# The first pair of blocks from half tables: loads into them, gathers by halves, and the next loads moved to GpSimd

## The chip, the cores and the metric

The kernel runs on one core of a Trainium2 chip. The metric is the device time of one execution in microseconds (us). Before the change three runs gave 733.4, 733.51 and 733.7; the median is 733.51. One further execution, under the profiler, took 733.14 with a span of 731.4 between its first and last instruction. All times below without a unit are microseconds from the start of that span.

## The reference: three layers of products of fields

The input x has 1024 rows of 39 fields with 64 numbers each. With X0 = x, each of three layers forms, for every row b and number e,

```
Xk_next[b, o, e] = sum over h, f of  Xk[b, h, e] * X0[b, f, e] * W[o, h, f]  +  bias[o]
```

with 64 outputs o. Each layer's result is summed over e, the three sums are put in a row of 192, and one linear layer (fc_w, fc_b) gives one number for each of the 1024 rows. Everything is float32.

The first layer has X0 twice, so its sum runs over pairs of fields. Because only sums over e and a linear layer follow, the last two layers are folded into weights beforehand: what is left for the large data is the first layer with its folded neighbour (128 output columns), a product with the first layer's result, and sums.

## The kernel before

**Blocks.** x is cut into 32 blocks of 32 rows. A block has 2048 columns (32 rows times 64 numbers) and one table row for each field, so it is a table of 39 rows of 8 KB, and a fortieth row of ones, which lets a single field pass as a product. Two blocks are a pair and share a DRAM table `xd[k]` of 80 rows (FT = 40 for each block); three such tables are used in turn.

**Gathers.** Products of all pairs of fields are made by multiplying differently ordered copies of the table. For each block, five tiles of 128 rows (`rt[n % 2]`, tiles 0 to 4) are filled with table rows in the orders that `lists` holds, one indirect DMA for each tile, issued by GpSimd (`gather_rows`, L174; called r in the profile). For each pair of blocks two smaller tiles, `ut` and `vt`, of 128 rows by 1024 columns, hold the few pairs of fields that the large tiles leave out (`roll_small`). Their 128 rows are four groups of 32, one for each combination of block and half of the columns.

**Products and matmuls.** Six products of tiles, numbered by `PAIRS = ((0, 1), (0, 2), (3, 1), (3, 2), (0, 4), (3, 4))`, are made by VectorE for each block (L219, `product`), each 128 by 2048, and one u by v product (L221) for each pair of blocks. TensorE multiplies each with its weights and sums into four PSUM banks for each block (L559, `multiply`). The u by v product is spread over both blocks by small matmuls (L579 and L590, `join`), between the two blocks of a pair. VectorE runs up to four products ahead of TensorE, with four buffers.

**Finishing a block.** `finish` takes the four banks: ScalarE copies one half and adds a column of fc_w (L607), VectorE adds the bias `b0s` and multiplies (L609), and sums over e (L620). In VectorE's order the finish of block 0 stands after product 3 of block 1 and ahead of product 4.

**Order of the queues.** Each engine runs its own instructions in the order in which the program lists them. An instruction waits until the tiles and DRAM rows that it needs are there; what stands behind it waits too. [...]

**The first pair.** The first block is handled by halves of 1024 columns. ScalarE's queue loads the halves of block 0 into `xh[0]` and `xh[1]` (39 rows each). GpSimd gathers tiles 0 to 3 of block 0 from them, eight half gathers, and among them issues the load of block 1 into `xd[0]`. SP copies both halves into `xd[0]` (L396). Tile 4, which needs the row of ones, u, v and the tiles of block 1 are gathered from `xd[0]`. Then GpSimd issues small loads of biases, b0s first (L477), and a row of ones. SP loads blocks 2 and 3 once TensorE's first step is in order, and later blocks 6 and up; GpSimd loads blocks 4 and 5 behind the gathers of blocks 2 and 3.

**The start.** Before the first product is used, TensorE, VectorE and ScalarE prepare the folded weights, up to the first L559 at 17.34.

Of the kernel before, what the change touches and what calls it, by code (L numbers as in the profile page):

```python
# [54 lines left out]
F32 = mybir.dt.float32  # L55
# [92 lines left out]
def cin_kernel(ctx: ExitStack, tc: tile.TileContext, x, w0t, b0, w1, b1, w2, b2, fc_w, fc_b, out):  # L148
# [11 lines left out]
    xd = [dram.tile([2 * FT, BLK], F32, name=f"xd{k}") for k in range(NTAB)]  # L160
    xh = [dram.tile([F, SUB], F32, name=f"xh{k}") for k in range(2)]

# [9 lines left out]

    def gather_rows(dst, table, k):
        nc.gpsimd.indirect_dma_start(  # L174
            dst, None, table, bass.IndirectOffsetOnAxis(ap=lists[:, k : k + 1], axis=0)
        )

    def roll(n, tiles=range(NT)):
# [4 lines left out]
    def roll_small(n):  # L183
        table = xd[n // 2 % NTAB].rearrange("f (t c) -> (f t) c", c=SUB)
        for k, dst in enumerate((ut, vt)):
            gather_rows(dst[n // 2 % 2], table, 2 * NT + k)

# [12 lines left out]

    lists = const.tile([128, 2 * NT + 2], I32, name="lists")
    rt = [const.tile([128, NT, BLK], F32, name=f"r{k}") for k in range(2)]
# [22 lines left out]
    with prep as prep:  # L225
# [25 lines left out]
        def load_half(k):  # L251
            nc.scalar.dma_start(
                xh[k].rearrange("f (b e) -> b f e", e=E), x[k * SB : (k + 1) * SB]
            )
# [34 lines left out]

        tmp = prep.tile([128, 16], F32, name="tmp")  # L290
        wide = prep.tile([128, 5, NT], F32, name="wide")
# [78 lines left out]

        fill_ones(0, nc.gpsimd, ones)


        nc.vector.tensor_scalar(unit, apart, 0, None, ALU.is_equal)
        for h in (0, H):
# [3 lines left out]
            )  # L379
        r, most, seat, far = (new() for _ in range(4))  # L380
        both_of = prep.tile([128, 2], F32, name="both_of")
# [7 lines left out]
        halves = [slice(0, SUB), slice(SUB, BLK)]  # L389
        for k, cols in enumerate(halves):  # L390
            for i in range(4):
                gather_rows(rt[0][:, i, cols], xh[k], i)
                if k and i == 1:
                    load(1, nc.gpsimd)
        for k in (1, 0):
            nc.sync.dma_start(xd[0][0:F, halves[k]], xh[k])  # L396
        roll(0, (4,))

# [31 lines left out]
        fused(seat, row, 96.0, seat, ALU.is_ge, ALU.add)  # L430
        step(row, 64.0, 2.0 * FT - 1.0, far)
        nc.vector.tensor_reduce(jumps, steps_at, AX.X, ALU.add)
# [28 lines left out]
        for k, n in enumerate((8, 5)):  # L461
            for t in range(2):
# [6 lines left out]
                )  # L469
        nc.vector.tensor_tensor(seat, seat, far, ALU.add)  # L470
        nc.vector.tensor_tensor(both_of[:, 0:1], most, jumps[:, 0:1], ALU.add)
        nc.vector.tensor_tensor(both_of[:, 1:2], both_of[:, 0:1], jumps[:, 1:2], ALU.add)
        nc.vector.tensor_scalar(lists[:, 2 * NT :], both_of, 2.0, seat, ALU.mult, ALU.add)
        roll_small(0)
        roll(1)
        for h in (0, H):
# [5 lines left out]
        )  # L482
        fill_ones(2, nc.gpsimd, ones)
        w1v = w1s.rearrange("o (h f) -> o h f", f=F)
# [82 lines left out]
    def join(n, p):  # L567
        open_block(n + 1)

        def tiles(t, side):  # L570
            rows = slice(SQUARE * t, SQUARE * t + SQUARE)
            return rows, po[n + t // 2][2 * t % 4 + side]

        for side in range(2):
            for t in range(4):
                for half in range(2):
                    rows, dst = tiles(t, side)
                    at = (side + half) * H
                    nc.tensor.matmul(  # L579
                        dst[half * H : half * H + H],  # L580
                        wa[rows, NPAIR, at : at + H],
                        p[rows, bass.ts(side, MM)],
                        start=t >= 2,
                        stop=t < 2 and half == side,
                    )
        for t in range(4):
            for side in range(2):
                rows, dst = tiles(t, side)
                half = (1 - side) * H
                nc.tensor.matmul(  # L590
                    dst[half : half + H],
                    wa[rows, NPAIR + 1, H : 2 * H],
                    ut[n // 2 % 2][rows, bass.ts(side, MM)],
                    start=False,
                    stop=t < 2,
                )
# [92 lines left out]
    for at, (n, c) in enumerate(steps[:-TAIL]):  # L689
        if c == 0 and 2 <= n and n + 4 < NBLK:  # L690
            load(n + 4)
# [15 lines left out]
        if not at:  # L707
            fields(0)
            nc.scalar.copy(ones1, ones)
            fill_ones(1, nc.sync, ones1)  # L710
            for k in (2, 3):
                load(k)
        if at == NPAIR - 2:
# [6 lines left out]
        if at + AHEAD < len(steps):  # L720
            n, c = steps[at + AHEAD]
            if at + AHEAD <= NPAIR:
                weight_rows(c)
            p[n, c] = product(n, c)
            if c == NPAIR - 1 and n + 2 < NBLK:
                roll(n + 2)
                if n % 2 == 0:
                    roll_small(n + 2)
                if n < 2:
                    load(n + 4, nc.gpsimd)  # L730
# [75 lines left out]
```

## Time and profile before

| What | Value |
|---|---|
| median of three runs | 733.51 us (733.4 to 733.7) |
| the profiled execution | 733.14 us, span 731.4 us |
| TensorE matmul busy | 724.7 us, 99% |
| VectorE busy | 638.3 us, 87% |
| GpSimd busy | 397.6 us, 54% |
| DMA moved | 197.24 MB, mean 270 GB/s |
| gathers from `xd` into r | 156, mean 1938 ns of GpSimd each |
| half gathers from `xh` into r | 8, mean 996 ns each |
| direct loads of a block by GpSimd | 3, mean 1055 ns each |

Busy time is the time in which an engine has an instruction in work; a share of 99% means that the engine hardly stood still. In the lists of instructions a row gives the start, how long it took, the engine (PE is TensorE, DVE is VectorE, ACT is ScalarE, POOL is GpSimd), the line of the program, the operation, what it writes and reads, and in brackets how long the engine was idle ahead of it and what ended that. "issue" there is time in which the profile shows nothing that the engine waits for. A group of a page has the count after x, then busy time and the mean of one in ns, then the idle time ahead.

### The profile page before, as it was taken

The numbers are of one execution on the slowest core, as the hardware profiler recorded it, in microseconds if no ns is written. First come the engines' busy times: TensorE is split into PE (matmuls) and PEld (weight loads), VectorE is DVE, ScalarE is ACT, GpSimd is POOL, SyncE is SP. The second block draws the span as 40 slices with busy tenths as digits, with TensorE's granted clock in tenths as the row PEclk, the third lists the DMA queues.
The fourth block names the chain that finished last, engine by engine and source line by source line (L and its number), as shares of the span: only waits on it lengthen the run. The fifth ranks groups of instructions, "written<-read, shape, count | busy, mean of one in ns | idle before, by whom it ended". The sixth has DMA issues, their size and how long they took to land.

```text
span 731.4 us, 6351 instructions
## 1 busy us (share of the span) xinstructions
PE 724.7 (99%) x2375; PEld 316.1 (43%) x2375; DVE 638.3 (87%) x521; ACT 166.9 (23%) x240; POOL 397.6 (54%) x254
## 2 busy tenths in 40 slices
PE   8999999999999999999999999999999999999998
PEld 4444444444444444444444444444444444444443
DVE  6999798988889988889988889888898988889885
ACT  3332121222212222221222212222121221212222
POOL 6789886536555445754537555455654547545300
PEclk9999999999999999999999999999999999999999
DMA  8997899789575887757679675896767777565700
GB/s 268 376 337 280 315 342 356 290 307 338 232 273 231 281 336 286 270 225 285 269 288 330 223 289 219 304 348 236 268 256 274 301 287 266 224 252 236 288 0 0
DMA packets 65983, 197.24 MB, mean 270 GB/s; under 512 B 40110, under 2 KB 40179, under 8 KB 45984
## 3 DMA queue, kind: packets, MB, share of 16 engines
q0 software_dynamic: 28784, 185.56, 65.5%
q1 hardware_dynamic: 35468, 9.29, 5.5%
q10 hardware_dynamic: 1700, 1.99, 1.0%
q8 instruction: 18, 0.29, 0.1%
q14 instruction: 13, 0.11, 0.0%
HBM read 196.76 MB, written 10.60 MB: 284 GB/s over the span
## 4 chain that ended last, share of the span: by engine, by line
PE 99%; DVE 0%; DMA 0%; issue 0%; ACT 0%; DVEq 0%
PE po L559 91%; PE po L579 4%; PE po L590 2%; PE idle L279 0%; PE pv L406 0%; PE pt L487 0%; PE small L323 0%; PE pv L487 0%; PE pw L418 0%; DMA fcrow<-in_fc_w 0%; PE tr L543 0%; DVE g L609 0%; DVE pairs L526 0%; DVE sums L631 0%; ACT z L607 0%
## 5 line engine op out<-in xcount | busy, mean ns | idle before, releaser
L559 PE MATMUL po<-p,wa 128*128 128x512 f32 x1536 | 666.0, 594 | 0.0
L219 DVE TENSOR_TENSOR p<-r 128x2048 f32<-128x2048 f32 (+2 forms) x198 | 434.1, 2224 | 72.4 <-PE po L559 67.1
L559 PEld LDWEIGHTS po<-p,wa 128*128 128x128 f32 x1536 | 290.5, 190 | 371.7 <-issue 354.6
L174 POOL DMA_INDIRECT r<-xd,lists x156 | 302.3, 1938 | 267.1 <-issue 266.2
L607 ACT ACTIVATE z<-po,columns 64x512 f32<-64x512 f32 x128 | 87.3, 682 | 380.1 <-PE po L590 217.9
L609 DVE SCALAR_TENSOR_TENSOR g<-po,b0s,z 64x512 f32<-64x512 f32 x128 | 95.9, 749 | 9.3 <-ACT z L607 5.3
L602 ACT COPY g<-r 39x1024 f32<-39x1024 f32 x64 | 66.7, 1043 | 155.0 <-DVE sums L620 126.8
L620 DVE TENSOR_REDUCE sums<-g 103x16 f32<-103x1024 f32 x62 | 75.6, 1220 | 2.1
L174 POOL DMA_INDIRECT u<-xd,lists x16 | 38.9, 2432 | 7.5 <-issue 4.6
L174 POOL DMA_INDIRECT v<-xd,lists x16 | 38.5, 2403 | 4.9 <-issue 4.9
L579 PE MATMUL po<-p,wa 32*64 32x512 f32 x512 | 31.6, 600 | 0.0
L221 DVE TENSOR_TENSOR p<-u,v 128x1024 f32<-128x1024 f32 x16 | 19.5, 1218 | 0.0
L579 PEld LDWEIGHTS po<-p,wa 32*64 32x64 f32 x512 | 9.4, 131 | 20.2 <-issue 19.4
L590 PE MATMUL po<-u,wa 32*64 32x512 f32 x256 | 17.0, 587 | 0.0
L174 POOL DMA_INDIRECT r<-xh,lists x8 | 8.0, 996 | 4.8 <-DVE tmp L387 2.7
L590 PEld LDWEIGHTS po<-u,wa 32*64 32x64 f32 x256 | 5.7, 132 | 8.0 <-issue 8.0
L526 DVE TENSOR_TENSOR pairs<-both 128x2 f32<-128x2 f32 (+27 forms) x59 | 6.1, 171 | 0.2
L544 ACT COPY wa<-tr 128x128 f32<-128x128 f32 x8 | 2.1, 266 | 16.2 <-PE tr L543 16.2
L279 PE MATMUL idle<-const-float32-1.0 128*128 128x256 f32 (+1 forms) x8 | 4.0, 596 | 0.8 <-PEq L793 0.8
L543 PE MATMUL tr<-unit,pairs 128*128 128x128 f32 x8 | 2.4, 294 | 2.2 <-DVE pairs L526 2.2
L543 PEld LDWEIGHTS tr<-unit,pairs 128*128 128x128 f32 x8 | 1.2, 151 | 4.7 <-ACT pairs L524 2.7
L168 POOL DMA_DIRECT2D xd<-in_x x3 | 3.2, 1055 | 0.0
(97 smaller groups left out, 56.7 us busy)
## 6 DMA issues: line engine op xcount, KB each, us to landing
xd<-in_x SPq DMA_DIRECT2D x28, 312.0 KB
r<-xd,lists POOLq DMA_INDIRECT x156, 8.9
xd<-in_x POOLq DMA_DIRECT2D x3, 312.0 KB, 7.6
w2s<-in_w ACTq DMA_DIRECT2D x1, 624.0 KB
w1s<-in_w ACTq DMA_DIRECT2D x1, 624.0 KB
w0s<-in_w0t ACTq DMA_DIRECT2D x1, 380.2 KB
xh<-in_x ACTq DMA_DIRECT2D x2, 156.0 KB
xd<-xh SPq DMA_DIRECT2D x2, 156.0 KB
```

The costliest lines, as they stand in the source:

```text
L174: nc.gpsimd.indirect_dma_start(dst, None, table, bass.IndirectOffsetOnAxis(ap=lists[:, k : k + 1], axis=0))
L219: nc.vector.tensor_tensor(p[:, cols], r[:, i, cols], r[:, k, cols], ALU.mult)
L221: nc.vector.tensor_tensor(p[:, 0:SUB], ut[n // 2 % 2], vt[n // 2 % 2], ALU.mult)
L279: nc.tensor.matmul(idle[:, 0:cols], nc.const_aps.tensor(1.0, (128, 128), F32), nc.const_aps.tensor(1.0, (128, cols), F32), start=True, sto ...
L526: nc.vector.tensor_tensor(out, diagonal(a, b, sa, sb), diagonal(b, a, sb, sa), ALU.add)
L559: nc.tensor.matmul(po[n][m], wa[:, c, side : side + 2 * H], p[:, bass.ts(m, MM)], start=n % 2 == 0 and c == 0, stop=n % 2 == 1 and c == NP ...
L579: nc.tensor.matmul(dst[half * H : half * H + H], wa[rows, NPAIR, at : at + H], p[rows, bass.ts(side, MM)], start=t >= 2, stop=t < 2 and ha ...
L590: nc.tensor.matmul(dst[half : half + H], wa[rows, NPAIR + 1, H : 2 * H], ut[n // 2 % 2][rows, bass.ts(side, MM)], start=False, stop=t < 2,)
L602: nc.scalar.copy(gt[H : H + F], rt[n % 2][0:F, 0, bass.ts(m, SUB)])
L607: nc.scalar.activation(z[one], po[n][m][other], AF.Identity, bias=fc0s[other])
L609: return lambda: nc.vector.scalar_tensor_tensor(g[n][m // 2][0:H, at], po[n][m][one], b0s[one], z[one], ALU.add, ALU.mult)
L620: nc.vector.tensor_reduce(sums[:, b_at : b_at + SB], g[n][m // 2].rearrange("p (b e) -> p b e", e=E), AX.X, ALU.add,)
```

## The change

- The half tables `xh[0]` and `xh[1]` grow to 80 rows each: 40 for block 0 and 40 for block 1, of 1024 columns. GpSimd fills their rows of ones first (two small DMAs instead of one).
- After the eight half gathers of block 0, GpSimd loads block 1's two halves directly into them. SP's two copies to `xd[0]` are gone.
- Tile 4 of block 0, u, v and all five tiles of block 1 are gathered from the half tables: two gathers for each tile, one for each half; u and v by two gathers of 64 rows.
- The groups of 32 rows of u and v are ordered half first, block second (`tiles` in `join`, `lists`), with one list more for the first pair; VectorE has two more small instructions for it.
- The loads of blocks 2 and 3 leave SP's queue and are issued by GpSimd behind the gathers of block 1, ahead of the bias loads. Blocks 6 and 7 are loaded by GpSimd behind the gathers of blocks 4 and 5; SP begins with block 8. The row of ones of `xd[0]` is filled later.

```diff
-    xh = [dram.tile([F, SUB], F32, name=f"xh{k}") for k in range(2)]
+    xh = [dram.tile([2 * FT, SUB], F32, name=f"xh{k}") for k in range(2)]
...
     def gather_rows(dst, table, k):
+        at = lists[0 : dst.shape[0], k : k + 1]
         nc.gpsimd.indirect_dma_start(
-            dst, None, table, bass.IndirectOffsetOnAxis(ap=lists[:, k : k + 1], axis=0)
-        )
+            dst, None, table, bass.IndirectOffsetOnAxis(ap=at, axis=0)
+        )
+
+    def roll_half(n, i, h):
+        k = n * NT + i
+        rows = F if n == 0 and i < NT - 1 else (n + 1) * FT
+        gather_rows(rt[n][:, i, bass.ts(h, SUB)], xh[h][0:rows], k)
...
     def roll_small(n):
-        table = xd[n // 2 % NTAB].rearrange("f (t c) -> (f t) c", c=SUB)
         for k, dst in enumerate((ut, vt)):
-            gather_rows(dst[n // 2 % 2], table, 2 * NT + k)
+            if n:
+                table = xd[n // 2 % NTAB].rearrange("f (t c) -> (f t) c", c=SUB)
+                gather_rows(dst[n // 2 % 2], table, 2 * NT + k)
+            else:
+                for h in range(2):
+                    gather_rows(dst[0][h * H : h * H + H], xh[h], 2 * NT + 2 + k)
...
-        fill_ones(0, nc.gpsimd, ones)
-
+        for k in range(2):
+            nc.gpsimd.dma_start(
+                xh[k][F::FT].rearrange("r (p c) -> p r c", c=128), ones[0:8]
+            )
...
-        for k, cols in enumerate(halves):
-            for i in range(4):
-                gather_rows(rt[0][:, i, cols], xh[k], i)
-                if k and i == 1:
-                    load(1, nc.gpsimd)
-        for k in (1, 0):
-            nc.sync.dma_start(xd[0][0:F, halves[k]], xh[k])
-        roll(0, (4,))
+        for at in range(8):
+            roll_half(0, at % 4, at // 4)
+        for k in range(2):
+            nc.gpsimd.dma_start(
+                xh[k][FT : FT + F].rearrange("f (b e) -> f b e", e=E),
+                xv[:, BB + k * SB : BB + (k + 1) * SB, :],
+            )
+        for k in range(2):
+            roll_half(0, 4, k)
...
-        nc.vector.tensor_tensor(seat, seat, far, ALU.add)
+        nc.vector.tensor_scalar(half_seat, seat, float(FT), None, ALU.mult)
+        fused(seat, seat, 2.0 * FT, far, ALU.mult, ALU.add)
...
-        nc.vector.tensor_scalar(lists[:, 2 * NT :], both_of, 2.0, seat, ALU.mult, ALU.add)
+        nc.vector.tensor_scalar(lists[:, 2 * NT + 2 :], both_of, half_seat, None, ALU.add)
+        nc.vector.tensor_scalar(
+            lists[:, 2 * NT : 2 * NT + 2], both_of, 2.0, seat, ALU.mult, ALU.add
+        )
         roll_small(0)
-        roll(1)
+        for i in range(NT):
+            for k in range(2):
+                roll_half(1, i, k)
+        for n in (2, 3):
+            load(n, nc.gpsimd)
...
-        fill_ones(2, nc.gpsimd, ones)
+        for k in (2, 0):
+            fill_ones(k, nc.gpsimd, ones)
...
-            return rows, po[n + t // 2][2 * t % 4 + side]
+            return rows, po[n + t % 2][t // 2 * 2 + side]
...
-                        start=t >= 2,
-                        stop=t < 2 and half == side,
+                        start=t % 2 == 1,
+                        stop=t % 2 == 0 and half == side,
...
-                    stop=t < 2,
+                    stop=t % 2 == 0,
...
-        if c == 0 and 2 <= n and n + 4 < NBLK:
+        if c == 0 and 4 <= n and n + 4 < NBLK:
             load(n + 4)
...
-            for k in (2, 3):
-                load(k)
...
-                if n < 2:
+                if n < 4:
                     load(n + 4, nc.gpsimd)
```

More of the change, by code (lines that the diff above doesn't have):

```diff
@@ L199, in cin_kernel @@
     kfin = const.tile([NY * 32, 1], F32, name="kfin")
-    lists = const.tile([128, 2 * NT + 2], I32, name="lists")
+    lists = const.tile([128, 2 * NT + 4], I32, name="lists")
     rt = [const.tile([128, NT, BLK], F32, name=f"r{k}") for k in range(2)]
@@ L252, in load_half @@
             nc.scalar.dma_start(
-                xh[k].rearrange("f (b e) -> b f e", e=E), x[k * SB : (k + 1) * SB]
+                xh[k][0:F].rearrange("f (b e) -> b f e", e=E), x[k * SB : (k + 1) * SB]
             )
@@ L287, in cin_kernel @@
         spin()
-        tmp = prep.tile([128, 16], F32, name="tmp")
+        tmp = prep.tile([128, 18], F32, name="tmp")
         wide = prep.tile([128, 5, NT], F32, name="wide")
@@ L379, in cin_kernel @@
             )
-        r, most, seat, far = (new() for _ in range(4))
+        r, most, seat, far, half_seat = (new() for _ in range(5))
         both_of = prep.tile([128, 2], F32, name="both_of")
@@ L430, in cin_kernel @@
         fused(seat, row, 96.0, seat, ALU.is_ge, ALU.add)
-        step(row, 64.0, 2.0 * FT - 1.0, far)
+        step(row, 64.0, 1.0 - 2.0 * FT, far)
         nc.vector.tensor_reduce(jumps, steps_at, AX.X, ALU.add)
```

## The prediction

> **What bounds the kernel now.** I read the page first, then the chain that ended last, then the timelines of GpSimd and VectorE over the first 70 us. From the page:
>
> ```profile
> span 731.4 us, 6351 instructions
> PE 724.7 (99%) x2375; PEld 316.1 (43%) x2375; DVE 638.3 (87%) x521; ACT 166.9 (23%) x240; POOL 397.6 (54%) x254
> L559 PE MATMUL po<-p,wa 128*128 128x512 f32 x1536 | 666.0, 594 | 0.0
> L219 DVE TENSOR_TENSOR p<-r 128x2048 f32<-128x2048 f32 (+2 forms) x198 | 434.1, 2224 | 72.4 <-PE po L559 67.1
> L174 POOL DMA_INDIRECT r<-xd,lists x156 | 302.3, 1938 | 267.1 <-issue 266.2
> ```
>
> TensorE has the end: its product matmuls (L559) never waited. VectorE mostly waits for TensorE. The chain shows where that begins and how one block passes:
>
> ```profile
> 17.34 1.82 PE po L559 x2
> ...
> 42.20 0.86 PE po L590 x16
> 43.06 41.40 PE po L559 x96
> ```
>
> Before 17.34 the weights are prepared. After it TensorE has no gap, so nothing behind 17.34 can be shortened by feeding it sooner; only the 17.34 us ahead could shrink. What the change can do is starve it. (The first matmul took 1.82 us where later ones take 0.86: TensorE's clock was granted at half from 16.9 to 20.3, after the pause at 14.3 to 16.4.)
>
> Block 1 starts at 43.06 and takes 3.45 us a product (41.40/12), so its fifth product, (1,4), is due at 56.86. Does the feed have room? GpSimd:
>
> ```profile
> 14.45 1.06 POOL L168 DMA_DIRECT2D xd<-in_x  x1
> 18.65 1.66 POOL L174 DMA_INDIRECT r<-xd,lists  x1 [0.30 <-issue]
> 23.23 0.94 POOL L174 DMA_INDIRECT u<-xd,lists  x1 [2.92 <-DVE p L219]
> 27.00 3.09 POOL L174 DMA_INDIRECT r<-xd,lists  x1 [0.30 <-issue]
> 30.39 2.61 POOL L174 DMA_INDIRECT r<-xd,lists  x1 [0.31 <-issue]
> 33.30 2.70 POOL L174 DMA_INDIRECT r<-xd,lists  x1 [0.30 <-issue]
> 37.64 1.16 POOL L477 DMA_DIRECT2D b0s<-in_b  x2
> 51.80 12.45 POOL L174 DMA_INDIRECT u<-xd,lists  x1 [0.30 <-issue]
> ```
>
> and VectorE:
>
> ```profile
> 29.77 2.28 DVE L219 TENSOR_TENSOR p<-r 128x2048 f32<-128x2048 f32 x1
> 32.88 2.28 DVE L219 TENSOR_TENSOR p<-r 128x2048 f32<-128x2048 f32 x1
> 46.84 1.53 DVE L609 SCALAR_TENSOR_TENSOR g<-po,b0s,z 64x512 f32<-64x512 f32 x2
> 52.35 11.09 DVE L219 TENSOR_TENSOR p<-r 128x2048 f32<-128x2048 f32 x5
> ```
>
> A gather takes 0.94 us and the next starts 0.30 later, 1.25 us in all, unless a product is running. The gather at 30.39 falls into the product that ends at 32.05 and ends 0.95 after it; the one at 33.30 falls into the one that ends at 35.16 and ends 0.84 after it; the one at 51.80 meets five products in a row, the last ending at 63.45, and ends 0.81 after that. So a gather that meets a product waits for its end, or for that of the whole row where the next product is ready, and then needs 0.81. The direct loads at 37.64 ran inside the product of 37.22 to 39.51 unhindered.
>
> [...] the gathers, which read their row numbers from SBUF, wait (12.45 us at 51.80); direct loads don't. [...] here the shortest gather took 4.6 us from start to landing (the first, 7.17 to 11.79), and I use 4.6. [...]
>
> **The change part by part.** *Removed:* SP's two copies xh to xd (312 KB; some 0.8 us of the DMA engines, at 10 to 17 us), and the load of block 1 between the gathers (1.06 + 0.30 us of GpSimd). Gathers seven and eight move up by 1.36 us, so VectorE loses its 0.72 us wait at 22.66. Worth nothing to TensorE, which doesn't wait there; it does remove the gap in which the u gather at 23.23 slipped in. *VectorE list arithmetic:* two more of 0.15 us at about 10 us, hidden by the 1.55 us that VectorE idles before 11.66. *The other numbering of the join* has the same matmuls and gathers: nothing; banks are wanted two matmuls earlier, and were free some 12 us before. *One more fill of ones* (0.7 us) sits in GpSimd's idle time before 7.17.
>
> *Added on GpSimd's queue.* Ahead of the bias loads (b0s) there were, after the eight halves, one gather of tile 4, u, v, and five of block 1: eight. Now there are 2 + 4 + 10 = 16, and two block loads of 1.06 taken over from SP. I charge a half gather, of 64 rows too, as a whole one: halves cost 0.94 in this trace. Step by step, products named (block, number):
>
> Half gathers end at 17.0. Two loads of 624 pieces, about 0.8 each (between 0.6 for a tiny one and 1.06 for 1248): 18.6. Tile 4, first half, behind the products that end at 19.48: 20.3. Second half, from 20.6: VectorE now runs four 1024-wide products in a row without a wait, from 20.31 to 24.95; it ends at 25.8 (22.3 if the row opens at its first seam). Then u first half, 26.1, behind (0,3) that ends at 28.2: 29.0. u second half 29.3 to 30.25, while VectorE waits for tile 4 (24.8 + 4.6 = 29.4). v first half, behind (0,4), 29.45 to 31.73: 32.6. v second half, behind (0,5), 32.6 to 34.9: 35.7.
>
> The v data land at 34.7 + 4.6 = 39.3, so the join's product runs 39.3 to 40.5 (before: 35.62 to 36.83); TensorE wants it at 40.30, 0.2 late. Meanwhile VectorE is idle and gathers run free: block 1's first four start at 36.05, 37.3, 38.5, 39.8, the last held to 41.3 by the join product. It lands at 40.4 + 4.6 = 45.0. Product (1,0) needs tiles 0 and 1 whole: 45.0 to 47.3, against 43.06 wanted. **First stall: 4.2 us.**
>
> The other six: 41.6, 42.85, 44.1 free; 45.35 held to 48.1 by (1,0), 48.4 to 50.6 by (1,1), 50.9 to 51.85. Two block loads: 53.95. b0s at 54.0 instead of 37.64. Landing: direct loads took from 5.0 (a lone x load) to 7.5 us; TensorE's wait makes the queue thin, I take 5.5: 59.5. On VectorE the first finishing instruction of block 0 (L609) needs b0s, and behind it in order stand the rest of that finish, 5.5 us (46.84 to 52.35), and product (1,4), 2.25: it is done at 67.25, against 56.86. **Second stall; in all TensorE is 10.4 us late.** The first is contained in this, not added, with its half clock: VectorE's chain to 67.25 doesn't pass through TensorE. After the second, of about 5 us, I add one window of half clock: 3.4 us long, in which half the work is done, so +1.7.
>
> Later: block 2's gathers start at about 58.7, after GpSimd's last small loads; its first two tiles land by 67.2, and (2,0) is wanted at 74.7. u and v of the second pair are shut out again by a row of products, as at 51.80 before, and I find them 4 us ahead of need. x of blocks 4 to 7 loaded by GpSimd comes a pair ahead. So no third stall.
>
> Sum against the profiled execution: 733.14 (span 731.4 + 1.7 around it) + 10.4 + 1.7 = 745.2. The median shown, 733.51, is 0.4 above that execution, so **745.5**.
>
> **Bounds of the unknown.** Low: if the row at 20.31 opens early and both halves of u slip in between, b0s goes out at about 50.5, lands at 56, and the delay is 56 + 7.75 − 56.86 = 6.9, no clock loss: 740. High: two more gathers held for a product each (4.5 us) and two half-clock windows: 10.4 + 4.5 + 3.4 = 18: 751.
>
> **Rivals.** *GpSimd keeps its pace* (no change): were no gather held, u would start once the block's load has landed, at about 24.2 (issued at 17.0; before, 14.45 to 23.23, with more queued ahead), and 14 gathers at 1.25 plus the loads' 2.1 put b0s at 43.8, landed at 49.3; (1,4) done at 57.05, 0.2 late: 733.7. For it: halves read as few row numbers, and gaps do occur (48.08 to 51.5). Against: every gather of the trace that met a product waited. *Only the first stall* (bias loads land in time, by about 49): 4.2 + 1.7, 739.4. Against: even ten free gathers from 36.05 and the loads put b0s at 50.6. *Faster*: fewer DMA ahead of the weights bring the first matmul forward. Its place is the start before 17.34; its price at most the half-clock loss plus a small wait, some 2 us: 731.5. It decides if the weights' landing sets the start; but the chain there is matmuls and VectorE back to back, and its only transfer is the small row fcrow (0.73 to 2.28), which the change leaves alone; the copies removed begin only at 10.1. *Worse still*: block 2 late as well, over 751.
>
> **How the numbers follow.** Forecast (both stalls, 740 to 751) 0.72; only the first stall 0.09; worse 0.06; no change 0.09; faster 0.04. About 0.2% (1.5 us) is what a measurement of this kernel can tell from no change. Slower 0.87, same 0.09, faster 0.04. The range 739 to 750 leaves out the last two, and the worst.
>
> **What the profile after would show.** Right: b0s starting after 48 us; L609 of block 0 waiting for a DMA for several us at about 50 to 60; TensorE idle once near 43 and longer near 60, with a half-clock slice after it; half gathers of 2 to 4 us in the stretch of 20 to 36. Wrong: half gathers of 0.94 throughout and b0s before 44, or the first matmul before 16.5. The forecast falls if held gathers get in at the seams between products.

## The result and the profile after

Six runs of the changed kernel gave a median of 742.45 us (740.53 to 747.0); six of the kernel before, beside them, 733.45 (732.02 to 733.82). The ratio is 1.0133, with a 95% interval of 1.0105 to 1.0161: the change makes the kernel slower by about 9 us. The profiled execution took 742.11 us with a span of 740.3, which is 8.9 more than the span before.

From the page of the kernel after (the page's head, the busy times, and TensorE's largest group, whose last field is the idle time ahead of it and what ended it):

```profile
span 740.3 us, 6363 instructions
PE 724.6 (98%) x2375; PEld 315.1 (43%) x2375; DVE 638.7 (86%) x523; ACT 166.8 (23%) x240; POOL 412.6 (56%) x269
L581 PE MATMUL po<-p,wa 128*128 128x512 f32 x1536 | 668.0, 595 | 6.6 <-DVE p L229 6.6
```

TensorE has the same work as before (724.6 us against 724.7). What is new is the wait: 0.0 us ahead of the product matmuls before (L559), 6.6 us after (L581), all of it for VectorE's products. Where these waits are, TensorE's timeline of the kernel after says. Its rows give the start, how long it took, the line and operation, and in brackets the idle time ahead of it:

```profile
40.35 1.98 PE L601 MATMUL po<-p,wa 32*64 32x512 f32 x32 [1.70 <-DVE p L231]
...
46.95 15.48 PE L581 MATMUL po<-p,wa 128*128 128x512 f32 x32 [3.77 <-DVE p L229]
...
65.31 27.73 PE L581 MATMUL po<-p,wa 128*128 128x512 f32 x64 [2.87 <-DVE p L229]
```

Three waits, all in the first two blocks: 1.70 us for the join's product and 3.77 for (1,0), which together are called the first stall below, and 2.87 for (1,4), the second stall. After 65.31 no product matmul waits. ScalarE's timeline confirms it: its first copy of a finished bank (L607 before, L629 after) comes at 43.06 and 43.18 for block 0, at 61.38 and 69.97 for block 1, at 721.18 and 729.77 for the last block. So block 0 ends on time, block 1 ends 8.6 us late, and the last block is late by the same 8.6.

What TensorE waited for is seen in VectorE's timeline of the kernel after:

```profile
39.07 1.23 DVE L231 TENSOR_TENSOR p<-u,v 128x1024 f32<-128x1024 f32 x1 [4.91 <-DMA v<-xh,lists]
...
44.61 2.29 DVE L229 TENSOR_TENSOR p<-r 128x2048 f32<-128x2048 f32 x1 [4.31 <-DMA r<-xh,lists]
...
57.46 1.53 DVE L631 SCALAR_TENSOR_TENSOR g<-po,b0s,z 64x512 f32<-64x512 f32 x2 [2.91 <-issue]
```

VectorE itself had nothing to do for 4.91 us until v was there, for 4.31 us until block 1's first two tiles were there, and for 2.91 us ahead of block 0's finish, whose bias b0s was late ("issue" means that the profile shows no releaser; that it is b0s, a later experiment shows). One step further back, GpSimd's timeline of the kernel after:

```profile
25.56 2.94 POOL L175 DMA_INDIRECT u<-xh,lists  x1 [0.30 <-issue]
28.80 2.61 POOL L175 DMA_INDIRECT v<-xh,lists  x1 [0.30 <-issue]
31.72 2.69 POOL L175 DMA_INDIRECT v<-xh,lists  x1 [0.30 <-issue]
34.71 0.94 POOL L175 DMA_INDIRECT r<-xh,lists  x1 [0.30 <-issue]
...
48.01 2.64 POOL L175 DMA_INDIRECT r<-xh,lists  x1 [0.30 <-issue]
...
52.59 1.23 POOL L498 DMA_DIRECT2D b0s<-in_b  x2
```

Three of the four half gathers of u and v take 2.6 to 2.9 us instead of 0.94 (the other, at 24.34, takes 0.92), block 1's first one starts at 34.71 instead of 25.73, and b0s goes out at 52.59 instead of 37.64. Meanwhile the DMA engines have less work. One stretch of the table by windows, first of the kernel before (the busy times are in the order TensorE, its weight loads, VectorE, ScalarE, GpSimd; the last three columns are the granted clock, the busy share of the DMA engines and GB/s):

```profile
24.00:34.00 10.00, 10.00 (x27) 4.46 (x26) 9.96 (x34) 1.52 (x8) 8.48 (x6) 1.00 1.00 353
```

and then of the kernel after:

```profile
24.00:34.00 10.00, 10.00 (x27) 4.39 (x26) 10.00 (x39) 1.71 (x12) 8.75 (x4) 1.00 0.47 150
```

GpSimd is as busy in both (8.48 and 8.75 of 10 us), but in the same 10 us the kernel before moves 3.5 MB and the kernel after 1.5 MB. A gather is called held here when it lasts until a product of VectorE has ended. Before, a held gather brought 1 MB (128 rows of 8 KB); now it brings 0.5 MB, or 0.25 MB for 64 rows of u or v.

### The profile page after: what moved, and what is told of

The parts are those of the page before. It is cut to its first block, busy times and chain, and to the rows that moved or that the text cites. A ratio compares the mean times of both kernels' runs of the same rounds, so it can differ in the third digit from the quotient of the medians.

```text
span 740.3 us, 6363 instructions
## 1 busy us (share of the span) xinstructions
PE 724.6 (98%) x2375; PEld 315.1 (43%) x2375; DVE 638.7 (86%) x523; ACT 166.8 (23%) x240; POOL 412.6 (56%) x269
## 4 chain that ended last, share of the span: by engine, by line
PE 91%; POOL 4%; DVE 2%; issue 2%; DMA 1%; ACT 0%; DVEq 0%
PE po L581 85%; PE po L601 4%; POOL r L175 2%; PE po L612 2%; DMA r<-xh,lists 1%; DVE p L229 1%; POOL v L175 1%; POOL u L175 1%; DVE g L631 0%; DMA b0s<-in_b 0%; POOL xd L168 0%; PE small L333 0%; DVE sums L642 0%; DVE sums L653 0%; ACT z L629 0%
## 5 line engine op out<-in xcount | busy, mean ns | idle before, releaser
L581 PE MATMUL po<-p,wa 128*128 128x512 f32 x1536 | 668.0, 595 | 6.6 <-DVE p L229 6.6
L175 POOL DMA_INDIRECT r<-xd,lists x150 | 309.9, 2066 | 258.4 <-issue 252.2
L581 PEld LDWEIGHTS po<-p,wa 128*128 128x128 f32 x1536 | 291.0, 191 | 379.7 <-issue 353.6
L629 ACT ACTIVATE z<-po,columns 64x512 f32<-64x512 f32 x128 | 87.4, 683 | 375.6 <-PE po L612 217.6
L175 POOL DMA_INDIRECT u<-xd,lists x15 | 26.6, 1772 | 4.6 <-issue 4.3
L175 POOL DMA_INDIRECT v<-xd,lists x15 | 26.5, 1768 | 4.6 <-issue 4.3
L175 POOL DMA_INDIRECT r<-xh,lists x20 | 24.5, 1224 | 7.7 <-issue 5.8
L168 POOL DMA_DIRECT2D xd<-in_x x6 | 6.3, 1062 | 0.0
L175 POOL DMA_INDIRECT v<-xh,lists x2 | 5.3, 2650 | 0.6 <-issue 0.6
L175 POOL DMA_INDIRECT u<-xh,lists x2 | 3.9, 1928 | 1.8 <-DVE p L229 1.5
```

Of the source, the lines that this page charges most:

```text
L168: engine.dma_start(xd[n // 2 % NTAB][first : first + F].rearrange("f (b e) -> f b e", e=E), xv[:, n * BB : (n + 1) * BB, :],)
L175: nc.gpsimd.indirect_dma_start(dst, None, table, bass.IndirectOffsetOnAxis(ap=at, axis=0))
L581: nc.tensor.matmul(po[n][m], wa[:, c, side : side + 2 * H], p[:, bass.ts(m, MM)], start=n % 2 == 0 and c == 0, stop=n % 2 == 1 and c == NP ...
L629: nc.scalar.activation(z[one], po[n][m][other], AF.Identity, bias=fc0s[other])
```

## The experiments

The theory to be tested: the loss comes from more places on GpSimd's queue (one place is one instruction), each of which a product of VectorE can hold for its whole length; so the first stall (v and block 1's tiles) and the second one (b0s) arise. The rivals: the moved loads, the amount or the row size of the data, the half-clock windows of TensorE, and that only one of the two stalls matters.

### The moved loads alone: no cost

The kernel before, with only the loads of blocks 2 and 3 moved.

```diff
         roll(1)
+        for n in (2, 3):
+            load(n, nc.gpsimd)
...
             fill_ones(1, nc.sync, ones1)
-            for k in (2, 3):
-                load(k)
```

> The kernel before, with the loads of blocks 2 and 3 issued by GpSimd behind the gathers of block 1 instead of by SP. Theory: b0s moves from 37.6 to about 39.8 and lands at about 47, up to 0.5 us after VectorE wants it at 46.8; product 4 of block 1 has 2.2 us to spare, so TensorE does not wait: 733.5 within 0.5. Rival (the moved loads are the cause): 740 or more.

Measured: 733.57 us, ratio 1.0004 (0.9985 to 1.0023). The two direct loads on GpSimd's queue cost nothing by themselves. In the kernel before they have room: b0s went out at 37.64 and was used at 46.84.

The opposite edit, on the changed kernel:

```diff
-        for n in (2, 3):
-            load(n, nc.gpsimd)
...
             fill_ones(1, nc.sync, ones1)
+            for k in (2, 3):
+                load(k)
```

> The changed kernel, with the loads of blocks 2 and 3 back on SP's queue where they stood before the change. Theory: b0s goes out two loads (2.0 us) earlier, at about 50.6, unless SP's pieces slow the gathers' data; the second wait of TensorE shrinks from 2.9 to about 1 us, the first two stay: 740 to 741. Rival (moving these loads behind the gathers is the cause): 734 to 735.

Measured: 741.83 us, ratio 1.0115 (1.0098 to 1.0132), 0.6 us less than the changed kernel and a little above the expected 740 to 741. The wait ahead of block 0's finish shrank to 0.45 us, the first stall was 1.60 + 3.97 us. The run does not isolate the second stall, because this execution's TensorE also began its products 2.2 us later (17.52 against 15.30), so there was less to wait for.

### Eight places without data

The kernel before, with eight gathers of 4 KB between v and block 1.

```diff
         roll_small(0)
+        for k in range(8):
+            nc.gpsimd.indirect_dma_start(
+                spare[:, k], None, xd[0][:FT].rearrange("f (t c) -> (f t) c", c=64),
+                bass.IndirectOffsetOnAxis(ap=lists[0:16, 0:1], axis=0),
+            )
         roll(1)
```

> The kernel before with eight more tiny gathers (16 rows of 64 columns, 4 KB each, into a tile that nobody reads) between v's gather and block 1's; nothing is left out. They move hardly any data but each is an instruction that reads row numbers. My theory (places on GpSimd's queue, held by products): the first goes at 25.7 free, three are held by the products that end at 29.1, 32.05 and 35.2, the rest run free; block 1's first gather starts at about 40.5 instead of 25.73 and its second ends at about 43 and lands at 47.5, so (1,0) is late by about 4 us and the bias loads by more: 739 to 743 us, the DMA share in 30 to 40 us far below 1. Rival one (the data of the transfers set the pace, not the places): no change, 733.5. Rival two (places cost 1.25 us each but are not held): block 1's first gather at 35.7, (1,0) at about 42: 733.5 to 735.

Measured: 745.97 us, ratio 1.0157 (1.0131 to 1.0183). GpSimd's timeline of this run:

```profile
30.44 2.59 POOL L477 DMA_INDIRECT spare<-xd,lists  x1 [0.31 <-issue]
...
41.41 0.95 POOL L174 DMA_INDIRECT r<-xd,lists  x1 [0.30 <-issue]
```

and TensorE's:

```profile
52.80 43.15 PE L565 MATMUL po<-p,wa 128*128 128x512 f32 x96 [8.05 <-DVE p L220]
```

A gather of 4 KB is held as long as one of 1 MB (2.59 us here, 2.61 at 30.39 in the kernel before), and block 1's first gather starts at 41.41, 0.9 after the time that was counted. The rivals "the data set the pace" and "places are not held" are out. The loss is 12 us, 3 more than the upper end of what was expected; the working had the landing too early. Block 1's first two tiles, issued at 41.41 and 42.67, were used at 50.45, not at 47.5. The DMA engines had stood at a busy share of 0.12 from 34 to 44; why the two tiles landed later than was counted is not shown. TensorE has one more wait that the expectation did not have, 1.26 us at 113.90, for a product of block 3.

### Block 1 by halves, alone

The kernel before, with only block 1's five gathers cut in two.

```diff
-        roll(1)
+        halved = xd[0].rearrange("f (t c) -> (f t) c", c=SUB)
+        for i in range(NT):
+            for h in range(2):
+                gather_rows(rt[1][:, i, bass.ts(h, SUB)], halved, 2 * NT + 2 + h * NT + i)
```

> The kernel before with only block 1's five gathers cut into halves (ten gathers of 4096-byte rows from the same full table, in the order of the changed kernel; two more small list instructions on VectorE at about 10 us). My theory: five more places between v and the bias loads, of which the second, third and fourth gather are held by the products that end at 29.1, 32.05 and 35.2; tiles 0 and 1 are issued by 36 and land at about 40.6, (1,0) is just in time; the bias loads go at about 45 and block 0's finish delays (1,4) by about 1 us: 733.5 to 735.5 us. Rival (halves of block 1 are themselves the whole loss): about 740.

Measured: 737.1 us, ratio 1.0044 (1.0023 to 1.0065), about 3 us. VectorE's timeline of this run:

```profile
45.17 2.29 DVE L219 TENSOR_TENSOR p<-r 128x2048 f32<-128x2048 f32 x1 [3.52 <-DMA r<-xd,lists]
```

and TensorE's:

```profile
47.51 10.57 PE L569 MATMUL po<-p,wa 128*128 128x512 f32 x24 [1.61 <-DVE p L219]
59.97 27.73 PE L569 MATMUL po<-p,wa 128*128 128x512 f32 x64 [1.89 <-DVE p L219]
```

The expectation had (1,0) just in time, and it was (39.35). It overlooked (1,1), which needs tile 2: VectorE waited 3.52 us for it, and TensorE 1.61. Block 0's finish and (1,4) follow on VectorE, so TensorE waited again, 1.89 us, for (1,4), although here b0s was in time.

Three places are held, as before (26.51, 29.90 and 32.80, each 2.6 to 3.1 us), but each brings half a tile. So tile 2 is complete with the sixth place and not with the third. GpSimd's timeline of this run, and VectorE's of the kernel before:

```profile
37.45 0.94 POOL L174 DMA_INDIRECT r<-xd,lists  x1 [0.30 <-issue]
```

```profile
39.80 2.29 DVE L219 TENSOR_TENSOR p<-r 128x2048 f32<-128x2048 f32 x1 [0.29 <-DMA r<-xd,lists]
```

Tile 2's last gather ended at 38.39 and VectorE used the tile at 45.17; before, it ended at 33.00 and the tile was used at 39.80. That is 6.8 us in both, so the later place accounts for the delay, and the landing behind it was no slower. The DMA share fell to 0.76 in 34 to 44 us, where the kernel before has 1.02; this goes with the held halves, and no cost of its own is shown. Five more places are worth 3 us, a third as much as the whole loss.

### No gather held: the stalls go, but the time does not come back

The changed kernel with one-input copies in place of block 0's products, which leaves their multiplication out. First for three of the products:

```diff
-            nc.vector.tensor_tensor(p[:, cols], r[:, i, cols], r[:, k, cols], ALU.mult)
+            if n == 0 and c > 2:
+                nc.vector.tensor_reduce(
+                    p[:, cols], r[:, k, cols].unsqueeze(2), AX.X, ALU.add
+                )
+            else:
+                nc.vector.tensor_tensor(p[:, cols], r[:, i, cols], r[:, k, cols], ALU.mult)
```

> The changed kernel, but products 3 to 5 of block 0 are made with one input: a reduction over one element that copies the second tile, of the same shape (the multiplication of these three is left out). Theory (a gather that meets a two-input product waits for its end): the four gathers of u and v start 1.25 us apart, the last by about 28.5 instead of 31.7, block 1's ten start by about 29.5, b0s goes out at about 44 to 45 instead of 52.6, product (1,0) is ready before TensorE wants it or within 1 us of it, and L631 of block 0 waits little: 733 to 736.5 us. Rival (the longer queue and the landing times alone do it, the products of VectorE hold nothing): u and v start as before at 24.3, 25.6, 28.8, 31.7 and the time stays at 742.

Measured: 741.15 us, ratio 1.0099 (1.0072 to 1.0125): the expected time was missed by far. GpSimd's timeline of this run:

```profile
20.70 5.27 POOL L175 DMA_INDIRECT r<-xh,lists  x1 [0.30 <-issue]
26.27 0.91 POOL L175 DMA_INDIRECT u<-xh,lists  x1 [0.30 <-DVE pairs L553]
```

From 26.27 to the join's product no gather is held, as expected, b0s goes out at 47.29, and TensorE has no second stall. But the edit left the four two-input products of 20.33 to 24.95 in place, and here tile 4's second half ran into them and was held for 5.27 us. TensorE's waits are others than in the changed kernel, 0.88 us ahead of a transpose of the last weights (at 40.12) and 1.92 within the join, and ScalarE's copy of that transpose came only at 45.38. How much of the miss is tile 4's and how much this late copy's, the run does not tell.

So the edit was widened to all of block 0's products of 1024 columns or more (`n == 0 and cols.stop - cols.start > MM`).

> The changed kernel with all of block 0's products of 1024 columns or more as one-input copies of the same size and duration; it leaves out the multiplication of those products. After the last two-input product of 512 columns (about 19.5) nothing holds a gather until the join's product. My theory (held gathers): both halves of tile 4 go by 23, u and v at 1.25 us apart until about 27, block 1's ten from 28 to 40, the bias loads at about 42; the join's product isn't late, (1,0) runs by 40: 733.3 to 735 us, within 0.3% of before. Rival (the half rows of 4096 bytes or the total of data are what is slow): the gathers go early but land late, the DMA engines stay full, (1,0) is still at about 42 to 45 and the time is 738 to 742.

And its control, the same edit in the kernel before:

> Control of the run with no holding: the kernel before with the same edit, block 0's products of 1024 columns or more as one-input copies; it leaves out their multiplication. If the edit itself is harmless, nothing in the kernel before is freed that mattered (TensorE did not wait), so 733.5 us, and the late copies of the last weights on ScalarE (2.5 and 4.9 us behind their transposes) belong to the changed kernel with its gathers bunched. If the edit itself brings these late copies: about 738 to 740 us with a gap of 3 to 4 us on TensorE near 40, and the run with no holding has to be read without that gap.

The control measured 732.45 us, ratio 0.9989 (0.9979 to 0.9999). GpSimd's timeline of the control:

```profile
26.94 0.94 POOL L174 DMA_INDIRECT r<-xd,lists  x1 [0.31 <-issue]
28.18 0.94 POOL L174 DMA_INDIRECT r<-xd,lists  x1 [0.30 <-issue]
```

These two gathers took 2.61 and 2.70 us in the kernel before. The products have the same length in both (2.27 us here, 2.28 there); with one input they hold nothing. Why, no run shows. And the kernel before gains next to nothing by it, since TensorE waited for nothing there (0.0 us ahead of L559).

In the changed kernel the same edit gave 739.83 us, ratio 1.0083 (1.0055 to 1.0112). GpSimd's timeline of that run:

```profile
29.77 0.94 POOL L175 DMA_INDIRECT r<-xh,lists  x1 [0.30 <-issue]
...
45.12 1.23 POOL L503 DMA_DIRECT2D b0s<-in_b  x2
```

and TensorE's:

```profile
43.51 0.33 PE L570 MATMUL tr<-unit,pairs 128*128 128x128 f32 x1 [3.55 <-issue]
```

All three stalls of the changed kernel are gone: the join's product runs at 34.67 (39.07 with holding), (1,0) at 38.85 (44.61), b0s goes out at 45.12 (52.59). So the held gathers are the cause of these stalls, and the rival that half rows land too late is out: it had (1,0) at 42 to 45. For the time the theory fails, and the 738 to 742 us of that rival were met by another way: only some 3 us came back (of 1.33%, 0.83% are left). In place of the three stalls there is a new one, 3.55 us ahead of a transpose of the last weights (L570), followed by a half-clock window from 44 to 47.4 (granted clock 0.50 from 44 to 46). ScalarE's copy of the transpose before it (L571) had come only at 43.07, 4.8 us after the engine was free, and the one before that 2.5 us after its transpose; the profile gives "remote" as what released them, which names no instruction. The control rules out the edit as the reason. One more run asks whether half gathers on end are enough for it: the kernel before with block 1 by halves and the one-input copies together.

> The kernel before with block 1's gathers in halves, and block 0's products of 1024 columns or more as one-input copies, so that no gather is held; it leaves out the multiplication of those products. With whole gathers the same copies cost nothing (control), with the changed kernel's half gathers 6 us and a gap of 3.6 us on TensorE. If ten half gathers on end are enough to bring that gap or a slower landing of rows of 4096 bytes: 736 to 739 us. If cutting the gathers costs only by the places that products hold: 732.5 to 733.5 us, and what was left in the run with no holding comes from another part of the change (u and v by halves, tile 4 by halves, the half tables).

Measured: 735.59 us, ratio 1.0037 (1.0022 to 1.0051). This lies between the two expectations, nearer the one in which half gathers on end are enough. Its profile is that of its slowest execution (738.45 us; the other four took 735.12 to 736.28), so the gap may be larger in it than in the others. ScalarE's timeline:

```profile
39.86 0.27 ACT L559 COPY wa<-tr 128x128 f32<-128x128 f32 x1 [9.41 <-remote]
```

TensorE's:

```profile
40.18 2.07 PE L574 MATMUL po<-p,wa 128*128 128x512 f32 x2 [3.70 <-ACT wa L559]
```

The transpose that this copy reads started at 33.60. So half gathers that are not held can bring the late copy, with the tables and everything else of the kernel before; with whole gathers and the same copies it did not come (control: transpose at 34.12, copy at 34.43). It isn't the load of the DMA engines alone: from 34 to 44 their share is 1.01 here and 1.02 in the kernel before, where no copy is late.

Nor is it the halves alone. In the run with eight places without data, five whole gathers follow one another unheld from 41.41 on, the join's last matmuls ended at 44.74, and ScalarE's first copy of a finished bank came 4.7 us after that. ScalarE's timeline of that run:

```profile
49.46 2.80 ACT L613 ACTIVATE z<-po,columns 64x512 f32<-64x512 f32 x4 [9.76 <-remote]
```

There TensorE waited for a product anyway. What ScalarE waits for in these microseconds is open.

### The second stall

Is the late b0s worth something of its own? First the five bias loads (b0s twice, b1s, b2s, fcb) were put ahead of the gathers on GpSimd's queue:

```diff
+        for h in (0, H):
+            nc.gpsimd.dma_start(b0s[h : h + H], b0.rearrange("(h o) -> h o", o=1))
...
         for at in range(8):
             roll_half(0, at % 4, at // 4)
```

> The changed kernel, with the five small bias loads issued right behind the rows of ones, in GpSimd's idle time ahead of the first gather. Theory (second stall: b0s lands late and the finish of block 0 stands ahead of product 4 of block 1 on VectorE): the 2.9 us that TensorE waits at 62.4 go, the waits at 38.6 (1.7) and 43.2 (3.8) stay, and so does the half clock after them: 2 to 3 us less than the changed kernel, about 739.5; the first gather may start up to 1.5 us later, which gives back at most that. Rival (product 4 of block 1 is late because its tile 4 lands late, not for b0s): the wait at 62.4 stays and the time stays at 742. Rival (b0s holds everything): back to 734.

Measured: 742.54 us, ratio 1.0137 (1.0117 to 1.0156): no gain. The second stall was gone, but the loads moved the first gathers from 7.10 to 8.28 and everything behind them, (1,0) ran at 46.91 instead of 44.61, and the first stall was 4.80 us; TensorE also waited 0.79 us at 16.16, since VectorE had waited 1.18 us for its first tiles. So all five were put on SP's queue, right behind `fcrow`, where nothing else is queued:

```diff
         nc.sync.dma_start(fcrow, fc_w)
+        for h in (0, H):
+            nc.sync.dma_start(b0s[h : h + H], b0.rearrange("(h o) -> h o", o=1))
...
```

> The changed kernel with the five bias loads on SP's queue at the start, where nothing else is queued, so that they are there long before they are needed and GpSimd's first gathers are not moved. My theory (two stalls add): the second stall of 2.87 us goes, the first stays at about 5.5 us: 739 to 740 us. Rival (the first stall alone sets the loss; the second only takes what a later one would): no gain, 742 us.

Measured: 740.06 us, ratio 1.0107 (1.0077 to 1.0138), within the expected 739 to 740 but for 0.06. TensorE's timeline of this run has one wait left in block 1, and a new one in block 3:

```profile
46.88 42.95 PE L581 MATMUL po<-p,wa 128*128 128x512 f32 x96 [5.27 <-DVE p L229]
...
107.44 27.73 PE L581 MATMUL po<-p,wa 128*128 128x512 f32 x64 [0.92 <-DVE p L229]
```

So b0s was what held block 0's finish. Its stall is worth about 2 us (against the kernel before, 7.2 us are left of the 9.0): block 1 ended 5.4 us late instead of 8.6, and 0.92 us were lost again in block 3, where the changed kernel does not wait. The first stall with its half-clock window is most of the loss.

### Nothing but gathers on GpSimd's queue

On top of that, block 1's half loads on SP at the start, and the loads of blocks 2 and 3 on SP in block 0:

```diff
+        for k in range(2):
+            nc.sync.dma_start(
+                xh[k][FT : FT + F].rearrange("f (b e) -> f b e", e=E),
+                xv[:, BB + k * SB : BB + (k + 1) * SB, :],
+            )
...
-        for n in (2, 3):
-            load(n, nc.gpsimd)
...
             fill_ones(1, nc.sync, ones1)
+            for k in (2, 3):
+                load(k)
```

> As the run with the bias loads on SP, and the two half loads of block 1 on SP at the start and the loads of blocks 2 and 3 on SP in block 0: GpSimd's queue now holds only gathers and fills. Seven loads are gone from it, nine places of gathers that were not there before remain. My theory (the extra gathers held by products are the loss): tile 4's halves go 1.7 us earlier, v and block 1's at most one product (3 us) earlier, the first stall shrinks to 2 to 5 us, no second: 736 to 740 us, still clearly slower than before. Rival (the loads on GpSimd's queue are the loss): 733.5 to 734.5.

Measured: 742.57 us, ratio 1.0124 (1.0101 to 1.0147). Neither the recovery of the theory nor that of the rival (the loads are the loss) came. GpSimd's timeline, from the slowest of its five runs (746.08 us):

```profile
16.25 0.94 POOL L175 DMA_INDIRECT r<-xh,lists  x1 [4.88 <-DMA r<-xh,lists]
...
22.76 5.27 POOL L175 DMA_INDIRECT r<-xh,lists  x1 [0.30 <-issue]
```

With block 1's x loaded at the start, the fifth half gather, the first of block 0's second half, waited 4.88 us, and tile 4's first half then ran into the row of four products. TensorE waited 1.09 us for weights and began its products only at 19.23. The queue was lighter by nine loads (the expectation counted seven), and what was won there was lost at its head. So the run does not decide about the rival; against it stands the run in which the moved loads alone cost nothing. Whether the fifth gather waited for the second half table, as it needs that first, or for an earlier gather's landing, as the profile has it, is not shown.

### TensorE's clock at the start

The kernel before has a half-clock window at 16.9 to 20.3 (granted clock 0.50 from 17 to 20), behind the 2.2 us in which TensorE idles. Four idle matmuls were put into that time:

```diff
                 stop=True,
             )
+        spin(4)
         for k, a in groups:
             nc.vector.transpose(
```

> The kernel before with four more idle matmuls of 256 columns on TensorE behind the last matmuls of the weights' preparation, in its idle time between 14.3 and 16.4; the output is the same. If the half-clock window at 16.9 to 20.3 comes from that idle time, it disappears and up to 1.7 us is gained: 731.8 to 732.8. Rival (VectorE's products and the landing of tiles set the pace of these microseconds anyway, or the window comes at another place): 733.5.

Measured: 733.98 us, ratio 1.0001 (0.9985 to 1.0017). TensorE's timeline of this run:

```profile
17.04 1.12 PE L560 MATMUL po<-p,wa 128*128 128x512 f32 x2
```

The window is gone (granted clock 1.00 from 16 to 21; two matmuls in 1.12 us, 2.02 before), and nothing is gained. In the timeline of ScalarE block 0 ends 0.66 us earlier than before and block 3 0.08 later: TensorE runs ahead a little and waits for its products a little later (0.47 us at 100.96). So this half-clock window costs nothing, since not TensorE but what feeds it sets the pace there. Apart from the control, which leaves work out, no version was faster than the kernel before.

## Why the prediction was right

The forecast of 745.5 us was 3 us above the 742.45 measured, in a range of 739 to 750, for the reason it gave: held gathers, two stalls of TensorE in the first two blocks, no third. By its own steps:

| Step | Predicted | Measured |
|---|---|---|
| half gathers end | 17.0 | 18.51 |
| block 1's loads end | 18.6 | 20.23 |
| tile 4, second half, ends | 25.8 (22.3 at a seam) | 22.85 |
| v, second half, ends | 35.7 | 34.41 |
| join's product | 39.3 to 40.5 | 39.07 to 40.30 |
| TensorE late at the join | 0.2 | 1.70 |
| block 1's gathers start | 36.05 | 34.71 |
| (1,0) | 45.0 to 47.3 | 44.61 to 46.90 |
| b0s goes out | 54.0 | 52.59 |
| block 0's finish starts | 59.5 | 57.46 |
| (1,4) done | 67.25 | 65.26 |
| half clock | 1.7, after the second stall | 3.03 us at half speed, after the first |

**The held gathers: right.** A half gather that met a product ended 0.8 to 0.9 us after that product, as worked out; half as many row numbers made it no shorter (64 rows of v took 2.61 and 2.69 us at 28.80 and 31.72, 128 rows in the kernel before 2.61 and 2.70 at 30.39 and 33.30). Two were counted on the wrong side: the eighth half gather, taken as free, took 2.29 us behind a product, and tile 4's second half, taken as held, slipped in at 21.85, at the first seam of a row of three products that began at 20.68 (the prediction named this seam as its low case; in the run with three one-input copies and in that with the loads on SP it was held, 5.27 and 5.25 us). The first cost 1.5 us, the second gave 3 back, and from v on GpSimd's queue ran 1.3 to 1.4 us ahead of the working.

**The first stall: right in place and cause, its size near by luck.** (1,0) was done 0.4 us ahead of the predicted time, because two errors cancel. The fourth half gather of block 1 was not held by the join's product and ended at 39.39, 1.9 us earlier than worked out; but it took 6.0 us from its start to landing, not the 4.6 that the prediction took from the fastest gather of the kernel before. TensorE, however, wanted it 1.8 us earlier than assumed, since its first product matmul came at 15.30 and not at 17.14; so the wait split in 1.70 ahead of the join and 3.77 ahead of (1,0), 5.5 against 4.2. The prediction had named a first matmul before 16.5 as a sign against it; but that the early start is the change's doing is not shown, for both kernels scatter: executions of the kernel before with one small edit started at 14.82, 15.65, 17.04 and 17.33, of the changed kernel with one edit at 15.51, 16.16, 17.36 and 17.55. In the profiled execution after, the first four of the weights' last matmuls (L509) took 1.34 us, in that before (L487) 2.36, though the granted clock is given as 1.00 in both there. What makes the starts scatter is not shown.

**The second stall: right in cause, mis-sized by 2 us.** (1,4) was done at 65.26, 8.4 us behind the 56.86 at which TensorE took it before; predicted were 10.4. The wait itself was 2.87 us, not about 5. The terms: b0s went out 1.4 us earlier, and the finish could start 4.9 us after that (52.59 to 57.46), not 5.5. That the first stall is contained in the delay of VectorE's chain, and not added to it, is right. The rival "only the first stall" was priced at 5.9 us above; the run with the bias loads on SP, which is this case, measured 7.2, of which 0.92 is the new wait in block 3. The rival "GpSimd keeps its pace" was priced at 733.7; the run in which all of block 0's large products are one-input copies measured 739.83. There b0s went out at 45.12, near the 43.8 of that price, and what it lacked is the wait at the late copies.

**The half clock: right in size, wrong in place.** It came behind the first stall, from 46.57 to 49.98, at a granted clock of 0.50, and cost half of the 3.03 us from 46.95 on, 1.5. Behind the second stall of 2.87 us there was none (granted clock 1.00 from 62 to 70), while the shorter pause of 2.2 us at the start of the kernel before was followed by one (0.50 from 17 to 20); so in this case the length of a pause alone does not decide, and what does is not shown. Ahead of (1,4) its cost is contained in the chain's delay as the first stall is: TensorE came to (1,4) later and waited there for less. (The 1.82 us that the prediction compares with 0.86 in the kernel before are those of two matmuls, not of one.)

**The sum.** On TensorE's side 3.77 + 2.87 + 1.5 make 8.1 of the 8.6 us by which block 1 ends late, while the early start and the wait at the join cancel within 0.2; on VectorE's side (1,4) is 8.4 late. The forecast's 10.4 + 1.7 was 3.5 above 8.6: 2.0 from the second stall's size and 1.7 from a window that did not follow it, less 0.2.

**What the prediction did not speak of** is the load of the DMA engines, which the held halves leave half idle (0.47 against 1.00). No run shows that this costs time of its own: the free half gathers of block 1 (34.71 to 38.45) landed 5.0 to 6.0 us after their start, that at 25.73 in the kernel before, free and whole, after 8.3.

**Not settled:** what the share of tile 4, u and v by halves is, since no run takes them alone; what the later load of block 1 costs (issued at 18.52 instead of 14.45; u's first gather at 24.34 instead of 23.23); and what makes ScalarE's copies late in some of the runs. The latter plays no part in the changed kernel itself, in whose profile these copies follow their transposes within 0.1 us.

## What to carry to other kernels

Count what is put on a queue in places as well as in bytes: where another engine can hold each place for a whole instruction, cutting a transfer in two leaves each hold as long as it was (here 2.6 to 3.1 us for whole gathers and for halves) and halves what it brings. To judge such a change, follow the queue to the last small thing behind it (here a bias of 256 bytes) and to its first user. And before a stall is priced, ask what TensorE would have waited for next: without the second stall of 2.9 us TensorE waited 0.9 us elsewhere, and 2 were won; the half clock at the start was worth nothing (ratio 1.0001 without it).

## What was not expected of the hardware

- A gather of 4 KB is held by a two-input product as long as one of 1 MB (2.59 and 2.61 us), and the same product with one input and the same length holds none (0.94 us).
- In some runs with gathers that follow one another unheld, copies on ScalarE came 2.5 to 6 us after the matmuls on TensorE that they read (33.60 and 39.86 with ten half gathers, 44.74 and 49.46 with five whole ones); in the control, with five whole gathers, they came within 0.4 us. No wait in the profile explains it.
- With 312 KB more to load ahead of the first half gathers, the fifth of them started after a wait of 4.88 us.
